# Moving softmax sums by DMA instead of transposing the attention outputs, in a fused FFN-attention-FFN layer

## The chip, the cores and the metric

The kernel runs on one core of one Trainium2 chip. The metric is the device time of one execution in microseconds, as the median of several runs. A profiled execution gives a trace beside it. In what follows PE is TensorE (matrix products and transposes by a product with the identity), DVE is VectorE, ACT is ScalarE, POOL is GpSimd, and SP is the queue from which most DMAs are issued. Each engine works its own instructions in program order.

## The reference, cut to what matters

The input `x` has 16 batches of 256 tokens with 256 features. The layer is

```
x = x + 0.5 * ffn(layernorm(x))        # 256 -> 1024 -> 256, ternary weights, exact gelu
x = x + attention(layernorm(x))        # 16 heads of 16, rotary, causal
x = x + 0.5 * ffn(layernorm(x))

q, k, v = x @ Wq.T, x @ Wk.T, x @ Wv.T      # heads of 16, q and k rotated
scores  = where(causal, q k^T / 4, -inf)
out     = softmax(scores) v                 # per head
return out @ Wo.T
```

All arithmetic is float32; the FFN splits its activations into a rounded part and a rest, so that two fast products stand for one exact one.

## The kernel before, in words

All tokens stay in SBUF (`xs`, 8 blocks of 512 tokens). The first FFN runs in 66 steps (8 blocks times 8 chunks of the hidden width, plus two): a step multiplies up one chunk (`up`), takes gelu twice on ACT, subtracts to get the rest on DVE or POOL (`h_rest`), and multiplies down the chunk of two steps before (`down`). The second FFN is alike.

Attention is a pipeline over batches, written out by hand in `slot(b, p)`: turn `b` has eight slots `p`. In one slot the scores of two heads of batch `b` are computed for their row maxima (tile `m`), and the transposed scores of two heads of batch `b - 1` for the weights (tile `w`). DVE takes the masked maxima out of `m`, adds the causal mask to `w`, and ACT takes exp into `pT`. Around the scores each slot holds another piece: turning the maxima (`turn_max`), the projections of the next batch (`project_qk`, `project_v`, `turn_x`), the rotary step on POOL (`rotate`, whose pairs of rows are swapped by two DMAs), `spread` on ACT, and what belongs to finished batches: `attend`, `divide`, `turn_out`, `project_out`, `add_out`, `last_stats`. The wrapper `InOrder` keeps every engine, SP's DMAs too, in the order in which the program is written. Since all instructions pass through it, the profile puts nearly everything on line 167, and groups are told apart by their tiles.

PSUM is shared by three pools of two tiles: `ps_w` (tile `w`, also the FFN's output), `ps_m` (tile `m`; a slot uses both), and `ps_mm` for all the rest. So a slot's maxima must be taken before the next slot's scores can be written, and a `mm` tile must be copied out before the next but one is begun.

`attend(b, half)` multiplies the weights with `vals`. Each head has 32 columns there: 16 values, a one, and zeros. The product therefore carries the head's outputs in 16 rows and the sum of its weights in a 17th. ACT copies it to `avs`. `divide(b, half)` transposes `avs` by four products with the identity, so that tokens lie in rows, takes the reciprocal of the 16 sums of a token and multiplies (tile `o`). `turn_out(b)` transposes `o` back by four more, and `project_out(b)` multiplies with `wo`. In `slot`, `attend` stands at slots 0 and 4, `divide` at 2 and 5, `turn_out` at 5, `project_out` at 7.

The list `head` lays the first projections and the first turn (`slot(0, 0..7)`) over the last 14 steps of the first FFN. After the last turn, a block of eight slots with weights alone (`ahead`, `behind`) finishes the last two batches, and `tail` finishes the last one inside the second FFN's first steps.

## Time and profile before

| | |
|---|---|
| median of 3 runs | 629.41 us (627.12 to 629.56) |
| the profiled execution's own time | 627.33 us |
| its span, first to last instruction | 625.5 us |
| first FFN | to about 166 us |
| attention, steady turns of 20.25 us | about 168 to 473 us |
| last two batches | 473 to 490 us |
| second FFN | from about 488 us |
| DVE busy in 300 to 325 us | 20.4 of 25 us |
| ACT busy in 300 to 325 us | 18.2 of 25 us |
| POOL busy in 300 to 325 us | 14.2 of 25 us |

A row of the groups gives the engine, the operation, output and input tiles, shapes, count, then busy time and the mean of one, then the engine's idle time just before them and what ended it. Rows in order of time give start, length, engine, operation and count. A product's rows overlap, because products are pipelined: their cost is the distance of their starts.

### The profile page before, as it was taken

Reading aid. Unit: us, or ns where it says so; the run is one execution under the profiler, and the core shown is the slowest. Engines: PE = TensorE matmul, PEld = TensorE weight load, DVE = VectorE, ACT = ScalarE, POOL = GpSimd, SP = SyncE. Lnnn points to the kernel's source line nnn. Section 1 sums busy time; section 2 is a strip of 40 time slices with the busy share of each in tenths; the row PEclk is TensorE's granted clock in tenths of the full one; section 3 lists DMA queues with packets and bytes.
Section 4 is the critical chain, followed back from the end, with each engine's and each line's share of the span. In section 5 each row is a group of like instructions: output and inputs, shape, how many; then the busy total and the mean of one; then the engine's idle time right before and its main releaser. Section 6 shows DMA issues by size and latency. Waiting matters only on the chain.

```text
span 625.5 us, 14708 instructions
## 1 busy us (share of the span) xinstructions
PE 601.8 (96%) x5580; PEld 488.6 (78%) x5580; DVE 463.6 (74%) x1658; ACT 414.5 (66%) x714; POOL 298.4 (48%) x270
## 2 busy tenths in 40 slices
PE   3999999989899999999999999999998999999997
PEld 3798999977677777777777777777766798888886
DVE  6877888865687988888888888888886465555553
ACT  3667666763567677767767676767765666766674
POOL 3545566572464466445654556453430243333343
PEclk9999999998999999999999999999999999999999
DMA  9800000000000001100100001100100011010001
GB/s 285 176 20 1 2 1 2 0 35 18 19 36 36 20 19 37 36 20 19 37 36 29 27 20 36 37 19 20 36 3 3 1 35 35 34 36 32 25 23 57
DMA packets 25478, 21.30 MB, mean 34 GB/s; under 512 B 10944, under 2 KB 21056, under 8 KB 25408
## 3 DMA queue, kind: packets, MB, share of 16 engines
q1 hardware_dynamic: 24848, 19.44, 9.9%
q8 instruction: 44, 0.72, 0.5%
q10 hardware_dynamic: 560, 0.92, 0.4%
q14 instruction: 26, 0.21, 0.1%
HBM read 7.51 MB, written 4.19 MB: 19 GB/s over the span
## 4 chain that ended last, share of the span: by engine, by line
PE 90%; DVE 5%; ACT 2%; issue 1%; DMA 1%; POOL 1%; DVEq 0%; SPq 0%; POOLq 0%
PE mm L167 37%; PE w L167 30%; PE m L167 23%; DMA w<-in_w1T_dram 1%; DVE h_rest L167 1%; DVE w2q L167 1%; ACT h_high L167 1%; DVE xn L167 0%; ACT h_whole L167 0%; DVE w L167 0%; DVE xn_a L167 0%; ACT pT L167 0%; DVE totals L167 0%; DVE st L167 0%; DVE w1q L167 0%
## 5 line engine op out<-in xcount | busy, mean ns | idle before, releaser
L167 DVE CUSTOM_DVE_ANT_0 masked<-m,mask_q 128x128 f32<-128x128 f32 x480 | 142.8, 353 | 40.5 <-PE m L167 39.3
L167 PE MATMUL m<-xnT,w1q 128*128 128x512 f32 x512 | 146.7, 408 | 1.1 <-DVE w1q L167 1.0
L167 ACT ACTIVATE h_high<-m,b_sb 128x512 fp32r<-128x512 f32 x128 | 88.1, 688 | 81.8 <-PE m L167 81.8
L167 DVE TENSOR_TENSOR h_rest<-h_whole,h_high 128x512 fp32r<-128x512 f32 x86 | 78.0, 908 | 73.3 <-ACT h_whole L167 72.8
L167 ACT ACTIVATE pT<-w 128x768 f32<-128x768 f32 x128 | 104.2, 814 | 30.3 <-DVE w L167 24.4
L167 PE MATMUL w<-qT,kT 32*128 32x256 f32 (+1 forms) x1024 | 121.1, 348 | 2.6 <-ACT pT L167 1.6
L167 PE MATMUL w<-w2q,h_high 128*128 128x256 f32 x480 | 121.4, 287 | 0.1
L167 PE MATMUL w<-w2q,h_rest 128*128 128x256 f32 x480 | 118.4, 280 | 1.3 <-DVE h_rest L167 1.3
L167 PEld LDWEIGHTS w<-qT,kT 32*128 32x128 f32 x1024 | 90.4, 184 | 34.1 <-issue 26.1
L167 PE MATMUL m<-kT,qT 32*128 32x128 f32 x960 | 114.9, 349 | 0.7 <-ACT kT L167 0.7
L167 POOL TENSOR_TENSOR h_rest<-h_whole,h_high 128x512 fp32r<-128x512 f32 x42 | 55.9, 1332 | 106.8 <-ACT h_whole L167 106.6
L167 PEld LDWEIGHTS m<-xnT,w1q 128*128 128x128 f32 x512 | 89.0, 192 | 17.5 <-DVE xnT L167 2.8
L167 PEld LDWEIGHTS w<-w2q,h_rest 128*128 128x128 f32 x480 | 91.0, 190 | 5.8 <-DVE h_rest L167 1.7
L167 DVE TENSOR_TENSOR w<-w,mask_k 128x512 f32<-128x512 f32 x128 | 88.8, 695 | 7.9 <-PE w L167 7.7
L167 PEld LDWEIGHTS w<-w2q,h_high 128*128 128x128 f32 x480 | 90.9, 189 | 4.5 <-DVE w2q L167 0.8
L167 ACT ACTIVATE h_whole<-m,b_sb 128x512 f32<-128x512 f32 x128 | 87.1, 681 | 0.0
L167 PEld LDWEIGHTS m<-kT,qT 32*128 32x128 f32 x960 | 66.0, 185 | 2.6 <-ACT kT L167 1.3
L167 POOL TENSOR_TENSOR w<-w,cosT 128x512 f32<-128x512 f32 x32 | 40.8, 1276 | 51.0 <-ACT w L167 33.1
L167 PE MATMUL mm<-xnT_a,wqk 128*128 128x256 f32 x256 | 62.2, 386 | 0.0
L167 POOL TENSOR_SCALAR var<-mv 128x4 f32<-128x4 f32 (+1 forms) x32 | 8.6, 268 | 109.6 <-DVE mv L167 109.1
L167 POOL TENSOR_TENSOR w<-w,sinT 128x512 f32<-128x512 f32 x32 | 41.3, 1291 | 32.5 <-DMA w<-w 32.5
L167 PEld LDWEIGHTS mm<-xnT_a,wqk 128*128 128x128 f32 x256 | 46.1, 190 | 7.6 <-issue 0.7
(86 smaller groups left out, 915.7 us busy)
## 6 DMA issues: line engine op xcount, KB each, us to landing
w<-w SPq DMA_DIRECT2D x64, 128.0 KB
out_dram<-x SPq DMA_DIRECT2D x15, 256.0 KB
x<-in_x_dram SPq DMA_DIRECT2D x7, 512.0 KB
w<-in_w2T_dram SPq DMA_DIRECT2D x1, 1024.0 KB
qT<-mT SPq DMA_DIRECT2D x64, 4.0 KB
w<-in_w1T_dram SPq DMA_DIRECT2D x1, 512.0 KB
w<-in_w1T_dram ACTq DMA_DIRECT2D x1, 512.0 KB
wqk<-in_wqkvT_dram SPq DMA_DIRECT2D x16, 32.0 KB
```

Source lines behind the costliest of these rows:

```text
L167: return tc.keep_in_program_order(getattr(self.engine, name)(*args, **kwargs))
```

## The change

Outputs are no longer turned to have tokens in rows. `vals` is filled with ones, and for every second group of four heads the 16 values lie in columns 16 to 31 instead of 0 to 15, the ones in the other half. So the product of `attend` has a head's outputs in 16 rows and its sum, repeated, in 16 rows beside them. ACT copies the product to `avs` as before and a second copy of its first half to `o`. Per batch, twelve DMAs of 16 rows (four in `gather` for each of three kinds) bring the outputs of a half together in `o` and the sums to the same rows in `over`, a part of the buffer that held the second weights. `divide`, called once a batch, takes the reciprocal of `over` (128x512) and multiplies it with `o` into `oT`, which is laid out for `project_out` at once. `wo` is loaded in the matching order of rows by eight DMAs. `turn_out` is gone, and so are the transposes of `divide`.

`gather` is issued in slots 0 to 3 of turn `b + 2`, `divide` runs in slot 1 of turn `b + 3`, `project_out` in slot 6 and `add_out` in slot 7 of that turn. `turn_x` moves from slot 6 to 2, `project_v` from 2 and 6 to 5 and 7, `project_qk`'s first half is split over slots 1 and 2, and `rotate` moves from slots 2 to 5 to slots 3 to 6. The head begins at step 40 instead of 46 and 52, its rotations are spread over steps 47 to 55, and the first turn begins at step 59 instead of 58, its last slot behind the FFN. In block 6 of the first FFN three `h_rest` move from DVE to POOL, and the addition of the bias moves to a later step.

```diff
-        nc.gpsimd.memset(v, 0.0)
-        nc.gpsimd.memset(v[:, :, :, HD : HD + 1], 1.0)
+        nc.gpsimd.memset(v, 1.0)
...
-            engine = gpsimd if f in (1, 3, 5) and not (ln == 0 and i >= NBLK - 2) else vector
+            engine = gpsimd if f in (1, 3, 5) and not (ln == 0 and i == NBLK - 1) else vector
...
-                if f == (0 if ln == 0 and i >= NBLK - 2 else 1 if ln == 2 and i == NBLK - 1 else 6):
+                if f == (1 if i == NBLK - 1 else 6):
                     add_bias(i)
...
-        scalar.copy(vals[b % 2][:, c, :, 0:HD], v.rearrange("p (h d) -> p h d", d=HD))
+        heads = "p (j e r d) -> p e j r d"
+        to = vals[b % 2][:, c].rearrange("p (j e r) d -> p e j r d", j=2, e=2)
+        for e in range(2):
+            scalar.copy(
+                to[:, e, :, :, e * HD : (e + 1) * HD],
+                v.rearrange(heads, j=2, e=2, d=HD)[:, e],
+            )
...
-        sums[b, half] = pp.tile([P, 2, S], FP, name="avs")
-        scalar.copy(sums[b, half], av)
...
+            sums[b] = pp.tile([P, 2, 2, S], FP, name="avs")
+            o[b] = pp.tile([P, 2, S], FP, name="o")
+        scalar.copy(sums[b][:, half], av)
+        scalar.copy(o[b][:, half, :], av[:, 0, :])
+
+    def gather(b, strips):
+        over[b] = spare[b % 2]
+        for r in strips:
+            first, second = (slice(at, at + HD) for at in (32 * r, 32 * r + HD))
+            sync.dma_start(out=over[b][first], in_=sums[b][second, :, 0, :])
+            sync.dma_start(out=over[b][second], in_=sums[b][first, :, 1, :])
+            sync.dma_start(out=o[b][second], in_=sums[b][second, :, 1, :])
+
+    def divide(b):
+        oT[b] = pp.tile([P, KC, S], FP, name="oT")
+        vector.reciprocal(over[b], over[b])
+        vector.tensor_mul(oT[b], o[b], over[b])
...
         if p == 0 and last is not None:
             attend(last, 1)
+            gather(last, (0,))
...
-            slots = VALUES.get(n, (2, 6))
+            slots = VALUES.get(n, (5, 7))
...
+        if p in (1, 2, 3) and up is not None:
+            project_qk(up, p // 3, {1: (0,), 2: (1,), 3: (0, 1)}[p])
+        if p in (1, 2, 3) and last is not None:
+            gather(last, (p,))
+        if p in (3, 4, 5, 6) and up is not None:
+            rotate(up, (p - 3) // 2, (p - 3) % 2)
...
-        if p == 6 and b + 2 < NB:
+        if p == 2 and b + 2 < NB:
             turn_x(b + 2)
+        if p == 6 and out is not None:
+            project_out(out, 0)
+            project_out(out, 1)
...
-        if p == 2 and last is not None:
-            divide(last, 1)
-        if p == 5 and past is not None:
-            divide(past, 0)
+        if p == 1 and out is not None:
+            divide(out)
...
+    head = {
+        40: lambda: ready_x(0, vector),
+        42: lambda: turn_x(0),
+        43: lambda: ready_x(1, vector),
+        44: lambda: project_qk(0, 0),
+        47: lambda: rotate(0, 0, 0),
+        48: lambda: (rotate(0, 0, 1), turn_x(1)),
+        50: lambda: project_qk(0, 1),
+        52: lambda: (rotate(0, 1, 0), spread(0, 0, 0)),
+        53: lambda: spread(0, 0, 1),
+        55: lambda: rotate(0, 1, 1),
+        56: lambda: ready_x(2, vector),
+    }
+    HEAD = 59
...
     ahead = {
-        0: lambda: (turn_max(z, 1), attend(a, 1)),
-        4: lambda: turn_out(a),
+        0: lambda: (turn_max(z, 1), attend(a, 1), gather(a, (0, 1, 2, 3))),
+        3: lambda: (project_out(y, 0), project_out(y, 1)),
         5: lambda: attend(z, 0),
-        6: lambda: project_out(a),
+        7: lambda: (project_out(a, 0), project_out(a, 1)),
     }
     behind = {
-        2: lambda: (divide(a, 1), last_stats(NB - 3)),
-        7: lambda: (add_out(a), last_stats(a), divide(z, 0)),
+        0: lambda: divide(y),
+        1: lambda: last_stats(y - 1),
+        4: lambda: add_out(y),
+        5: lambda: divide(a),
+        6: lambda: last_stats(y),
+        7: lambda: (add_out(a), last_stats(a)),
     }
...
     tail = [
-        lambda: attend(z, 1),
-        lambda: divide(z, 1),
-        lambda: turn_out(z),
-        lambda: project_out(z),
+        lambda: (attend(z, 1), gather(z, (0, 1, 2, 3))),
...
+        lambda: divide(z),
+        lambda: (project_out(z, 0), project_out(z, 1)),
         lambda: (add_out(z), last_stats(z)),
     ]
```

More of the change, by code (lines that the diff above doesn't have):

```diff
@@ L109 @@
             )
-    nc.sync.dma_start(out=wo, in_=woT.rearrange("(k p) f -> p k f", p=P))
+    for r in range(4):
+        for e in range(2):
+            at, to = 4 * HD * e + HD * r, 32 * r + HD * e
+            nc.sync.dma_start(
+                out=wo[to : to + HD, :, :],
+                in_=woT.rearrange("(k p) f -> p k f", p=P)[at : at + HD],
+            )
     nc.sync.dma_start(out=cos_sb, in_=rope_c.rearrange("(c p) d -> p c d", p=P))
@@ L409, in after_first @@
         later.extend(todo)
-    xn_a, xnT, qT, kT, o, oT, y_a = {}, {}, {}, {}, {}, {}, {}
-    pT, sums = {}, {}
+    xn_a, xnT, y_qk, qT, kT, o, oT, y_a = {}, {}, {}, {}, {}, {}, {}, {}
+    pT, sums, over = {}, {}, {}
     raw, pair = (
@@ L419 @@
     )
-    qk = [flat2[:, at : at + 2 * S].rearrange("p (n s) -> p n s", n=2) for at in (0, 2 * S)]
+    qk, spare = (
+        [flat2[:, at : at + 2 * S].rearrange("p (n s) -> p n s", n=2) for at in (k, k + 2 * S)]
+        for k in (0, 4 * S)
+    )
     def ready_x(b, engine=gpsimd):
@@ L436, in turn_x, with project_qk @@
         scalar.copy(xnT[b], tp)
-    def project_qk(b, j):
-        to = ps_mm.tile([P, 2, S], FP, name="mm")
-        for n in range(2):
+    def project_qk(b, j, parts=(0, 1)):
+        if 0 in parts:
+            y_qk[b, j] = ps_mm.tile([P, 2, S], FP, name="mm")
+        to = y_qk[b, j]
+        for n in parts:
             for k in range(KC):
@@ L449, in project_qk @@
                 )
+        if 1 not in parts:
+            return
         scalar.copy(raw[j], to)
@@ L483, in project_v @@
             )
-        scalar.copy(vals[b % 2][:, c, :, 0:HD], v.rearrange("p (h d) -> p h d", d=HD))
+        heads = "p (j e r d) -> p e j r d"
+        to = vals[b % 2][:, c].rearrange("p (j e r) d -> p e j r d", j=2, e=2)
+        for e in range(2):
+            scalar.copy(
+                to[:, e, :, :, e * HD : (e + 1) * HD],
+                v.rearrange(heads, j=2, e=2, d=HD)[:, e],
+            )
     def turn_max(b, j):
@@ L574, in attend @@
                     )
-        sums[b, half] = pp.tile([P, 2, S], FP, name="avs")
-        scalar.copy(sums[b, half], av)
-    def divide(b, half):
         if half == 0:
-            o[b] = pp.tile([P, 2, H, HD], FP, name="o")
-        tp = ps_mm.tile([P, 2, 8, 32], FP, name="mm")
-        for c in range(2):
-            for n in range(2):
-                tensor.transpose(
-                    tp[:, c, 4 * n : 4 * n + 4, :].rearrange("p h d -> p (h d)"),
-                    sums[b, half][:, n, c * P : (c + 1) * P],
-                    ident,
-                )
-        inv = pp.tile([P, 2, 8, 1], FP, name="inv")
-        vector.reciprocal(inv, tp[:, :, :, HD : HD + 1])
-        vector.tensor_mul(
-            o[b][:, :, 8 * half : 8 * half + 8, :],
-            tp[:, :, :, 0:HD],
-            inv.to_broadcast([P, 2, 8, HD]),
-        )
@@ L598, in turn_out @@
-    def turn_out(b):
-        tp = ps_mm.tile([P, KC, S], FP, name="mm")
-        for k in range(KC):
-            for c in range(2):
-                tensor.transpose(
-                    tp[:, k, c * P : (c + 1) * P],
-                    o[b][:, c, 8 * k : 8 * k + 8, :].rearrange("p h d -> p (h d)"),
-                    ident,
-                )
-        oT[b] = pp.tile([P, KC, S], FP, name="oT")
-        scalar.copy(oT[b], tp)
-    def project_out(b):
-        y = y_a[b] = ps_mm.tile([P, 2, D], FP, name="mm")
-        for c in range(2):
-            for k in range(KC):
-                tensor.matmul(
-                    y[:, c, :],
-                    oT[b][:, k, c * P : (c + 1) * P],
-                    wo[:, k, :],
-                    start=(k == 0),
-                    stop=(k == KC - 1),
-                )
+            sums[b] = pp.tile([P, 2, 2, S], FP, name="avs")
@@ new lines, in divide, with project_out @@
+    def divide(b):
+        oT[b] = pp.tile([P, KC, S], FP, name="oT")
+        vector.reciprocal(over[b], over[b])
+        vector.tensor_mul(oT[b], o[b], over[b])
+    def project_out(b, c):
+        if c == 0:
+            y_a[b] = ps_mm.tile([P, 2, D], FP, name="mm")
+        for k in range(KC):
+            tensor.matmul(
+                y_a[b][:, c, :],
+                oT[b][:, k, c * P : (c + 1) * P],
+                wo[:, k, :],
+                start=(k == 0),
+                stop=(k == KC - 1),
+            )
@@ L640, in slot @@
         up, now, past, last = (n if 0 <= n < NB else None for n in (b + 1, b, b - 1, b - 2))
-        if p == 0 and 0 <= b - 3 < NB:
-            add_out(b - 3)
+        out = b - 3 if 0 <= b - 3 < NB else None
+        if p == 7 and out is not None:
+            add_out(out)
         weigh = scores(bw, p, bm, p ^ 1)
@@ L645, in slot @@
             attend(last, 1)
+            gather(last, (0,))
         if p == 1 and past is not None:
             turn_max(past, 1)
-        if p == 5:
-            if now is not None:
-                turn_max(now, 0)
-            if last is not None:
-                turn_out(last)
+        if p == 5 and now is not None:
+            turn_max(now, 0)
         for n, at in ((past, p + 8), (now, p)):
-            slots = VALUES.get(n, (2, 6))
+            slots = VALUES.get(n, (5, 7))
             if n is not None and at in slots:
                 project_v(n, slots.index(at))
-        if p in (1, 3) and up is not None:
-            project_qk(up, p // 2)
-        if p in (2, 3, 4, 5) and up is not None:
-            rotate(up, p // 2 - 1, p % 2)
+        if p in (1, 2, 3) and up is not None:
[4 more added lines that the diff above has]
+            rotate(up, (p - 3) // 2, (p - 3) % 2)
         if p == 4 and past is not None:
             attend(past, 0)
-        if p == 6 and b + 2 < NB:
+        if p == 2 and b + 2 < NB:
             turn_x(b + 2)
+        if p == 6 and out is not None:
+            project_out(out, 0)
+            project_out(out, 1)
         if p == 7:
-            if last is not None:
-                project_out(last)
             if b + 3 < NB:
@@ L673, in slot @@
         weigh()
-        if p == 2 and last is not None:
-            divide(last, 1)
-        if p == 5 and past is not None:
-            divide(past, 0)
-        if p == 0 and 0 <= b - 3 < NB:
-            last_stats(b - 3)
+        if p == 1 and out is not None:
+            divide(out)
+        if p == 0 and 0 <= b - 4 < NB:
+            last_stats(b - 4)
         for n, at in ((up, {7: (0, 1)}), (now, {2: (1, 0), 3: (1, 1)})):
@@ L685, in slot @@
             later.pop(0)()
-    head = [
-        lambda: (turn_x(0), ready_x(1, vector)),
-        lambda: project_qk(0, 0),
-        lambda: (rotate(0, 0, 0), project_qk(0, 1)),
-        lambda: (turn_x(1), rotate(0, 0, 1), rotate(0, 1, 0), ready_x(2, vector)),
-        lambda: rotate(0, 1, 1),
-        lambda: (spread(0, 0, 0), spread(0, 0, 1)),
-    ] + [lambda p=p: slot(0, p) for p in range(8)]
+    head = {
[12 more added lines that the diff above has]
+    HEAD = 59
     begin, step, *_ = ffn(0, after_first)
@@ L702 @@
         step(u)
-        if u == (NBLK - 3) * NFC + 6:
-            ready_x(0, vector)
-        if u >= FFN_STEPS - len(head):
-            head[u - (FFN_STEPS - len(head))]()
+        head.get(u, lambda: None)()
+        if u >= HEAD:
+            slot(0, u - HEAD)
+    for p in range(FFN_STEPS - HEAD, 8):
+        slot(0, p)
     for b in range(1, NB - 1):
@@ L734 @@
     a, z = NB - 2, NB - 1
-    add_out(NB - 3)
+    y = NB - 3
     ahead = {
-        0: lambda: (turn_max(z, 1), attend(a, 1)),
-        4: lambda: turn_out(a),
+        0: lambda: (turn_max(z, 1), attend(a, 1), gather(a, (0, 1, 2, 3))),
+        3: lambda: (project_out(y, 0), project_out(y, 1)),
         5: lambda: attend(z, 0),
-        6: lambda: project_out(a),
+        7: lambda: (project_out(a, 0), project_out(a, 1)),
     }
     behind = {
-        2: lambda: (divide(a, 1), last_stats(NB - 3)),
-        7: lambda: (add_out(a), last_stats(a), divide(z, 0)),
+        0: lambda: divide(y),
[4 more added lines that the diff above has]
+        7: lambda: (add_out(a), last_stats(a)),
     }
@@ L751 @@
     tail = [
-        lambda: attend(z, 1),
-        lambda: divide(z, 1),
-        lambda: turn_out(z),
-        lambda: project_out(z),
+        lambda: (attend(z, 1), gather(z, (0, 1, 2, 3))),
+        lambda: None,
+        lambda: None,
+        lambda: None,
+        lambda: None,
+        lambda: divide(z),
+        lambda: (project_out(z, 0), project_out(z, 1)),
         lambda: (add_out(z), last_stats(z)),
```

## The prediction, made before the result was known

> **What bounds the kernel now.** I read the page's engine row and chain first.

> ```profile
> PE 601.8 (96%) x5580; PEld 488.6 (78%) x5580; DVE 463.6 (74%) x1658; ACT 414.5 (66%) x714; POOL 298.4 (48%) x270
> ...
> PE 90%; DVE 5%; ACT 2%; issue 1%; DMA 1%; POOL 1%; DVEq 0%; SPq 0%; POOLq 0%
> ```

> TensorE (PE) sets the end, but only as long as its in-order queue never waits. The stage that changes is attention, so next I read PE in order of time over one batch's turn (start, length):

> ```profile
> 301.11 0.48 PE L167 MATMUL w<-qT,kT 32*128 32x256 f32 x1
> ...
> 301.98 1.51 PE L167 MATMUL mm<-pT,vals 128*32 128x256 f32 x32
> 303.42 0.48 PE L167 MATMUL w<-qT,kT 32*128 32x256 f32 x1
> ...
> 304.29 0.44 PE L167 MATMUL mm<-ident,maxes 128*128 128x128 f32 x2
> 304.56 0.60 PE L167 MATMUL mm<-ident,o 128*128 128x128 f32 x4
> 305.19 0.66 PE L167 MATMUL mm<-ident,avs 128*128 128x128 f32 x4
> 305.77 0.48 PE L167 MATMUL w<-qT,kT 32*128 32x256 f32 x1
> ```

> Starts tell the cost, since the ends overlap: the scores of a slot take 0.87 us (301.11 to 301.98), attend 1.44, two maxes' transposes 0.27, four transposes about 0.56 (0.58 here, 0.53 elsewhere). The same list gives 0.97 for project_v, 1.92 for eight wqk or wo products. The turn is 20.25 us (301.11 to 321.36), all PE work. VectorE (DVE) in the same slots, and its groups:

> ```profile
> 303.20 0.69 DVE L167 TENSOR_TENSOR w<-w,mask_k 128x512 f32<-128x512 f32 x1
> 304.39 0.29 DVE L167 CUSTOM_DVE_ANT_0 masked<-m,mask_q 128x128 f32<-128x128 f32 x1 [0.49 <-PE m L167]
> ...
> 306.11 0.25 DVE L167 RECIPROCAL inv<-mm 128x16 f32<-128x16 f32 x1
> 306.39 0.42 DVE L167 TENSOR_TENSOR o<-mm,inv 128x256 f32<-128x256 f32 x1
> ```

> ```profile
> L167 DVE CUSTOM_DVE_ANT_0 masked<-m,mask_q 128x256 f32<-128x256 f32 x240 | 100.7, 420 | 0.0
> ...
> L167 DVE CUSTOM_DVE_ANT_0 masked<-m,mask_q 128x128 f32<-128x128 f32 x240 | 68.7, 286 | 40.5 <-PE m L167 39.3
> ...
> L167 DVE RECIPROCAL inv<-mm 128x16 f32<-128x16 f32 x32 | 7.9, 247 | 0.8 <-PE mm L167 0.8
> ```

> A slot asks DVE for four masked maxima (1.12 us, 302.08 to 303.20) and one mask addition (0.60), 1.72 in all. The pool of `m` has two tiles and a slot uses both, so PE's scores of slot p+1 cannot begin before DVE has read slot p's. Slots last 2.3 to 3.0 us: DVE has only 0.5 to 1.0 us to spare in each. A long DVE instruction stops PE.

> **What the change removes.** Twelve transposes a batch go (eight of `avs`, four of `o`): 3 x 0.56 = 1.7 us of PE. Summing the new slots 0 to 7 (scores, then attend; maxes + half wqk; half wqk + turn_x; full wqk; attend; maxes + project_v; wo; project_v): 2.31 + 2.10 + 2.37 + 2.79 + 2.31 + 2.12 + 2.80 + 1.85 = 18.65 us, 1.6 below 20.25. From DVE two short divisions go (2 x 0.65, start to start).

> **What it adds on DVE.** One reciprocal of 128x512 and one product of 128x512, back to back behind slot 1's mask addition. The product is like the 128x512 addition: 0.69. Call the reciprocal R. The trace has it only for 16 elements: 247 ns. Other DVE instructions that read PSUM have a fixed part near 150 ns (286 ns at 128 elements and 420 at 256 make 1.05 ns an element, leaving 152; a 128x1 operation on PSUM takes 151). The remaining 97 ns over 16 elements is 6.1 ns an element, so R = 0.15 + 512 x 6.1 ns = 3.26 us. From below: if the 97 ns are a latency paid once, R = 0.15 + 512 x 1.05 ns = 0.69 (0.8 with it). [...]

> **What this does to a turn.** Let T0 be the start of slot 0's scores. Masked maxima start 0.95 after a slot's scores. Slot 0: they end at 2.07, mask addition 2.67, last_stats 1.08 (as at 313.62 to 314.70): DVE free at 3.75. Slot 1 starts at 2.31, its maxima could start at 3.26 but do at 3.75; they end 4.87, mask addition 5.47, then R + 0.69: DVE free at 6.16 + R. Slot 2's scores have run meanwhile, their maxima end at 7.28 + R, and slot 3's scores are held until about 0.12 before that (w products go first). Without waits slot 3 starts at 2.31 + 2.10 + 2.37 = 6.78. So PE stands still for 7.16 + R - 6.78 = 0.38 + R in slots 1 to 2. Slot 7 is now so short (1.85, with add_out's 0.69 before its maxima) that slot 0 waits another 0.1. The turn is 18.65 + 0.1 + 0.38 + R = 19.13 + R. The same reckoning on the kernel before gives 20.25, as measured. With R = 3.26 it is 22.39, +2.14 us; 13 turns (b = 3 to 15) have a division: **+27.8 us**. Queued behind the reciprocal are the masked maxima (PE waits), slot 2's mask addition and thus its exp on ScalarE.

> **The clock.** Before the first turn, PE idled 1.35 and 1.90 us close together and then ran at half clock (columns: stretch, length, busy of the engines, granted clock):

> ```profile
> 140.00:141.00 1.00, 0.00 (x0) 0.00 (x0) 1.00 (x2) 0.00 (x0) 1.00 (x1) 1.00 0.00 0
> 141.00:142.00 1.00, 0.70 (x8) 0.55 (x8) 0.75 (x2) 0.00 (x0) 0.07 (x1) 1.00 0.00 0
> 142.00:143.00 1.00, 1.00 (x5) 0.73 (x3) 0.74 (x5) 0.00 (x0) 0.00 (x0) 0.65 0.00 0
> 143.00:144.00 1.00, 1.00 (x4) 0.74 (x3) 0.46 (x4) 0.00 (x0) 0.00 (x0) 0.50 0.00 0
> 144.00:145.00 1.00, 1.00 (x7) 1.00 (x6) 0.00 (x0) 0.84 (x2) 0.00 (x0) 0.50 0.00 0
> 145.00:146.00 1.00, 1.00 (x8) 0.78 (x9) 0.54 (x1) 0.42 (x1) 0.00 (x0) 0.65 0.00 0
> ```

> That is about 3.4 us at half, 1.7 us lost. [...] The row shows that partly idle stretches suffice. [...]

> **What it adds elsewhere.** ScalarE: two more copies of 128x256 in attend (2 x 0.37), project_v's copy in two pieces (about 0.27 each for 0.37), less oT's copy (0.585): +0.5 us on some 14 busy in 20; the exp waits for DVE anyway, so 0. If that cover is gone, 0.5 x 14 = 7 us. SP: twelve more DMAs a turn. Issues of the pair and qT DMAs take about 0.55 us each, so 6.6 us of a queue that issued eight a turn. Three go into each of slots 0 to 3, ahead of a pair or qT DMA, which is at most 1.65 us late; pair DMAs land 2.7 us after issue (316.95 to 319.65), the rotation is a slot later and spread in slot 7, so 0 here. The sums are divided a turn after they were moved: 0. GpSimd's moved rotations: 0 in the steady turn.

> **Head, first turns, end.** The head's stalls before the first turn (1.35 + 1.90 + 1.65 of half clock = 4.9) come from DVE behind two xn_a normalizations slowed to 2.67 us and h_rest at 4.59 for two, all beside GpSimd's rotations. Those spread over steps 40 to 56, three h_rest go to GpSimd, and the scores start a step later: **-4** (-5 to +2; GpSimd's sum of 17 us in eleven steps of 1.9 is near full). Turns 1 and 2 lose four and twelve transposes and wo's 1.92, which goes into the last block: -0.53 - 3.53 = **-4.1**. The last block (eight slots of scores alone, 472.7 to 489.4): two reciprocals stand in it; following mask addition, exp and the two `w` tiles slot by slot, its last exp ends 19.9 us after its start instead of 16.7: **+3.3**. Tail: eight transposes less (-1.1), a DVE block of 3.9 us at step 5 against some 3 us of slack of h_rest (+0.6): **-0.5**.

> Sum: 27.8 + 10.4 - 4 - 4.1 + 3.3 - 0.5 = +32.9 on the profiled execution's 627.3 (span 625.5): **660 us**. The runs' median is 629.4, 0.3% above it, inside the spread.

> **Rivals.** *A fast reciprocal* (R = 0.69): turn 19.82, 13 x -0.43 = -5.6, no half clock, last block -1, the rest -8.6: -15, **612 us**. For it: a latency could explain 97 ns. Against: no other short row has 80 ns more. Break-even lies at 13 (R - 1.12) + 1.67 (R - 0.68) - 1 = 8.6, R = 1.7 us, 3 ns an element. [...] *No clock loss at R = 3.26*: **650**; it belongs to my likeliest case. *Late DMAs:* if the pair DMAs behind three gathers cost 1.65 us in each of 14 turns, +23: **683**; SP's idle time and the slack above speak against it. *In between* (R = 1.4 to 2.2): 623 to 640.

> **How the numbers follow.** R near 3.3 with or without the clock: 0.62, 650 to 672. Eight cycles: 0.15. Fast: 0.14. In between: 0.06, half of it the same as before. Late DMAs: 0.03. Leaving out the fast case below and the extremes above gives 638 to 684. A measurement here tells about 0.5% from no change: faster 0.15, same 0.03, slower 0.82.

> **What would show it.** RECIPROCAL 128x512 near 3.3 us; an idle PE of about 3 us in slot 2 to 3 of each turn, released by DVE `maxes`; turns of 22 to 23.5 us; dips of the granted clock in attention; no SP wait on the way; PE matmuls fewer by 192. A reciprocal under 1.7 us makes the forecast wrong.

## The result, and the profile after

The changed kernel takes 724.55 us (median of 4 runs, 723.64 to 726.30) against 629.23 us for the kernel before (4 runs beside it): 1.152 times as long, with a 95% interval of 1.148 to 1.155. The forecast was 660, with a range of 638 to 684. The direction was right; the slowdown was three times the one forecast.

The engine row and the chain's row of the page after:

```profile
PE 652.8 (90%) x5388; PEld 503.8 (70%) x5388; DVE 503.2 (70%) x1623; ACT 414.7 (57%) x762; POOL 302.0 (42%) x271
...
PE 69%; DVE 15%; ACT 5%; DMA 4%; issue 2%; SPq 2%; POOL 1%; DVEq 0%; POOLq 0%
```

PE has 192 products fewer and is yet busy 51 us longer, which says that products ran more slowly. On the chain DVE has gone from 5% to 15%, ACT from 2% to 5%. The two new groups on DVE:

```profile
L174 DVE RECIPROCAL w<-w 128x512 f32<-128x512 f32 x16 | 53.5, 3342 | 0.0
...
L174 DVE TENSOR_TENSOR oT<-o,w 128x512 f32<-128x512 f32 x16 | 11.2, 699 | 0.5
```

So R = 3.34 us, where 3.26 was forecast, and 0.70 for the product. The disputed term was right. To find where the rest went, the two traces are laid side by side at five marks: the transposes of the maxima in slot 1 of batches 1 and 3, the last scores for maxima, and the first `up` product of the second FFN.

| stretch | before | after | difference | forecast |
|---|---|---|---|---|
| start to slot 1 of batch 1 | 171.27 | 169.07 | -2.2 | -4 |
| turns 1 and 2 | 41.57 | 40.57 | -1.0 | -4.1 |
| turns 3 to 15, to the last scores for maxima | 257.04 | 348.83 | +91.8 | +38.2 |
| from there to the second FFN (last block) | 18.20 | 23.45 | +5.3 | +3.3 |
| second FFN | 137.42 | 140.58 | +3.2 | -0.5 |
| sum (spans 625.5 and 722.5) | | | +97.0 | +32.9 |

The turns hold nearly all of it. A steady turn lasts 27.30 us (from one reciprocal to the next, 348.12 to 375.42), 7.05 more than before; 2.94 were forecast. One stop of PE in order of time, first PE, then DVE (start, length, the idle time before and what ended it in brackets):

```profile
350.00 0.69 PE L174 MATMUL w<-qT,kT 32*128 32x256 f32 x2
352.79 0.37 PE L174 MATMUL m<-kT,qT 32*128 32x128 f32 x1 [2.10 <-DVE maxes L174]
...
354.93 3.78 PE L174 MATMUL mm<-xnT_a,wqk 128*128 128x256 f32 x8
```

```profile
348.12 3.34 DVE L174 RECIPROCAL w<-w 128x512 f32<-128x512 f32 x1
351.49 0.69 DVE L174 TENSOR_TENSOR oT<-o,w 128x512 f32<-128x512 f32 x1
352.10 0.28 DVE L174 CUSTOM_DVE_ANT_0 masked<-m,mask_q 128x128 f32<-128x128 f32 x1
...
375.42 3.34 DVE L174 RECIPROCAL w<-w 128x512 f32<-128x512 f32 x1
```

PE's slot 3 begins at 350.00 and stops, until DVE, behind the reciprocal and the product, takes the maxima of slot 2 from 352.10 on. PE resumes at 352.79. This is the wait that was forecast, in its place; its idle time is 2.10 us by PE's products and 2.50 by its weight loads, where 0.38 + R = 3.7 was reckoned. But the eight `wqk` products after it take 3.7 us (354.93 to the next start at 358.64). In the kernel before they took 1.93:

```profile
319.43 1.99 PE L167 MATMUL mm<-xnT_a,wqk 128*128 128x256 f32 x8
321.36 0.48 PE L167 MATMUL w<-qT,kT 32*128 32x256 f32 x1
```

The windows of the changed kernel over the same time (stretch, length, busy of PE, PEld, DVE, ACT and POOL, granted clock, DMA share and GB/s) tell why:

```profile
351.00:352.00 1.00, 0.00 (x0) 0.00 (x0) 0.97 (x2) 0.00 (x0) 0.59 (x1) 1.00 0.26 54
...
353.00:354.00 1.00, 1.00 (x13) 0.74 (x12) 0.90 (x3) 0.06 (x1) 0.02 (x1) 0.58 0.47 156
354.00:355.00 1.00, 1.00 (x8) 0.35 (x3) 0.39 (x3) 1.00 (x2) 1.00 (x1) 0.50 0.18 41
...
359.00:360.00 1.00, 1.00 (x16) 0.92 (x12) 0.00 (x0) 1.00 (x3) 0.00 (x0) 0.51 0.00 0
360.00:361.00 1.00, 1.00 (x26) 0.64 (x24) 0.75 (x5) 0.93 (x3) 0.00 (x0) 1.00 0.35 131
```

After the wait PE runs at a granted clock of 0.50 for about 6.8 us (353.15 to 359.98), in which it does 3.4 us of work: up to 3.4 us lost, in every turn, where the forecast had 0.8. A second wait is new and was not in the forecast at all. Slot 0 begins late (PE, then ACT):

```profile
342.68 0.37 PE L174 MATMUL m<-kT,qT 32*128 32x128 f32 x1 [0.79 <-ACT kT L174]
```

```profile
341.30 0.43 ACT L174 COPY vals<-mm 128x128 f32<-128x128 f32 x2 [1.24 <-PE mm L174]
341.62 0.52 ACT L174 ACTIVATE qT<-w,own 128x256 f32<-128x256 f32 x1
342.03 0.60 ACT L174 ACTIVATE kT<-w,one,own 128x256 f32<-128x256 f32 x1
```

The scores of a new batch need `kT`, which `spread(up, 0, 0)` writes in slot 7. There it stands behind the two copies of `vals`, and these wait for `project_v`, which now runs in slot 7. Slot 7 itself has become short (1.85 us). PE's idle at this place is 0.79 us by its products and 1.2 by its weight loads.

### The profile page after: what moved, and what is told of

The parts are those of the page before. It is cut to its first block, busy times and chain, and to the rows that moved or that the text cites. A ratio compares the mean times of both kernels' runs of the same rounds, so it can differ in the third digit from the quotient of the medians.

```text
span 722.5 us, 14732 instructions
## 1 busy us (share of the span) xinstructions
PE 652.8 (90%) x5388; PEld 503.8 (70%) x5388; DVE 503.2 (70%) x1623; ACT 414.7 (57%) x762; POOL 302.0 (42%) x271
## 4 chain that ended last, share of the span: by engine, by line
PE 69%; DVE 15%; ACT 5%; DMA 4%; issue 2%; SPq 2%; POOL 1%; DVEq 0%; POOLq 0%
PE mm L174 27%; PE m L174 21%; PE w L174 21%; DVE w L174 8%; DMA w<-avs 3%; SPq L174 2%; DVE oT L174 1%; DVE masked L174 1%; ACT kT L174 1%; ACT qT L174 1%; ACT vals L174 1%; DMA w<-in_w1T_dram 1%; ACT avs L174 1%; ACT h_high L174 1%; DVE w2q L174 1%
## 5 line engine op out<-in xcount | busy, mean ns | idle before, releaser
L174 PE MATMUL m<-kT,qT 32*128 32x128 f32 x960 | 144.5, 392 | 39.7 <-DVE maxes L174 29.3
L174 PE MATMUL w<-qT,kT 32*128 32x256 f32 (+1 forms) x1024 | 153.4, 385 | 4.9 <-ACT pT L174 4.0
L174 PEld LDWEIGHTS w<-qT,kT 32*128 32x128 f32 x1024 | 104.3, 204 | 46.4 <-issue 27.8
L174 PEld LDWEIGHTS m<-kT,qT 32*128 32x128 f32 x960 | 84.0, 210 | 57.4 <-DVE maxes L174 41.1
L174 DVE TENSOR_TENSOR h_rest<-h_whole,h_high 128x512 fp32r<-128x512 f32 x83 | 71.2, 858 | 73.9 <-ACT h_whole L174 73.4
L174 POOL TENSOR_TENSOR h_rest<-h_whole,h_high 128x512 fp32r<-128x512 f32 x45 | 60.1, 1336 | 109.4 <-ACT h_whole L174 109.2
L174 PE MATMUL mm<-xnT_a,wqk 128*128 128x256 f32 x256 | 87.6, 490 | 0.0
L174 PEld LDWEIGHTS mm<-xnT_a,wqk 128*128 128x128 f32 x256 | 57.9, 242 | 22.0 <-ACT pT L174 7.2
```

Of the source, the lines that this page charges most:

```text
L174: return tc.keep_in_program_order(getattr(self.engine, name)(*args, **kwargs))
```

## The experiments

Theory: the length of one DVE instruction in one slot stops PE (R + 0.48 a turn), and the stop halves PE's clock for some microseconds after it; slot 0's wait on `kT` comes on top. Rivals: the twelve DMAs are late; ScalarE's added copies; DVE's sum of work; the half clock comes from something else.

### The reciprocal made short, `spread` made early, and both

`e1_r16` inverts only 16 of the 512 columns, so the outputs are multiplied with sums instead of their inverses; `e2_spread6` lays `spread` one slot earlier; `e4_r16_spread6` has both.

```diff
-        vector.reciprocal(over[b], over[b])
+        vector.reciprocal(over[b][:, 0, 0:16], over[b][:, 0, 0:16])
```

```diff
-            if up is not None:
-                spread(up, 0, 0)
+        if p == 6 and up is not None:
+            spread(up, 0, 0)
```

> The changed kernel, but the reciprocal takes only 16 of the 512 columns (the other sums are left as they are, so the output is not the layer's). Theory: the reciprocal of 3.34 us causes both the wait of TensorE in slots 2 and 3 and the two windows of half clock behind it. Then its turn falls from 27.3 us to 19.13 + 0.25 by the prediction's formula plus 1.2 for the new wait of slot 0 on kT, about 20.6 us, the granted clock in attention is 1.00, and the whole takes about 628 us. Rival (the twelve DMAs or the moved pieces are the cost): the turn stays above 25 us and the whole above 695 us.

> The changed kernel with the first spread of the next batch in slot 6 instead of 7, so that slot 0's scores of maxima need not wait for kT behind the copies of the values. If the parts of a turn simply add, the turn falls by 1.2 us to 26.1 and the whole by 16 us to about 708 us. [...]

> Both: reciprocal of 16 columns only (output not the layer's) and the first spread in slot 6. By the formula 19.13 + 0.25 = 19.4 us a turn, TensorE never long idle, whole about 613 us: the most that the freed TensorE time could have given with a short division. Rival (a further wait is hidden in the new order of slots): turn above 20.2 us, whole not below 625 us.

Measured, in one execution each: 638.2, 693.8 and 623.3 us. The reciprocal's length alone is worth 86 us. Without it, and with `spread` early, the turns are shorter than in the kernel before, though all twelve DMAs, both copies and all other moves are there. The turn in `e1_r16`, then the turn and its windows in `e4_r16_spread6`:

```profile
253.89 0.24 DVE L174 RECIPROCAL w<-w 128x16 f32<-128x16 f32 x1
...
274.95 0.24 DVE L174 RECIPROCAL w<-w 128x16 f32<-128x16 f32 x1
```

```profile
250.92 0.24 DVE L174 RECIPROCAL w<-w 128x16 f32<-128x16 f32 x1
...
270.58 0.24 DVE L174 RECIPROCAL w<-w 128x16 f32<-128x16 f32 x1
```

```profile
270.00:280.00 10.00, 10.00 (x121) 7.27 (x118) 8.10 (x41) 7.60 (x14) 4.61 (x5) 1.00 0.28 82
280.00:290.00 10.00, 10.00 (x125) 7.32 (x129) 9.06 (x42) 6.91 (x15) 6.39 (x7) 1.00 0.08 18
```

A turn takes 21.06 us in the first and 19.66 in the second (250.92 to 270.58), so the wait on `kT` costs 1.40 us. In the second PE is busy all the time at full clock, 0.59 us a turn faster than the kernel before. So the turns are near the 20.6 and 19.4 that were expected. The whole times are not: both lie 10 us above the theory. In `e1_r16` the turns and a second FFN of 140.4 us explain most of it; in `e4_r16_spread6` there is half clock from 449.9 to 456.7 in the last turn, and twice more in the last block.

`e2_spread6` did not agree with the expectation that the parts add (26.1, and 708 for the whole): its turns last 24.40 or 25.9 us, 1.64 and 3.1 more than the 22.76 that the long reciprocal alone gives (19.66 + 3.10). One and the same kernel has one half-clock stretch in some turns (24.40) and two in others (25.9); a turn of 24.40 shows one half-clock stretch of about 3.4 us (a granted clock of 0.90, 0.50, 0.50, 0.50 and 0.90 in the five windows of 1 us from 339 to 344).

### PE kept busy during the wait

`e3_warm` and `e6_warm6` add products whose result nobody reads, at the end of slot 2 (twelve and six calls; each is two instructions):

```diff
+    def idle(b):
+        to = ps_mm.tile([P, 2, D], FP, name="mm")
+        for n in range(6):
+            tensor.matmul(
+                to[:, n % 2, :], ident, wo[:, n % 2, :], start=True, stop=True
+            )
...
+        if p == 2 and out is not None:
+            idle(b)
```

> The changed kernel with twelve 128x256 products that nobody reads at the end of slot 2, where TensorE otherwise waits for the maxima behind the reciprocal. They keep it busy for about 2.9 us. Theory (half clock follows from the wait): no half clock behind slot 2, the turn falls by 3.4 us to about 23.9 us or a little more, the whole to 675 to 690 us, although more work is done. Rival (the clock is lowered by something else, such as the whole load, or the products only add): the turn stays or grows, 725 us or more.

> The changed kernel with six products of ident with wo (512 columns in all a pair, result unused) at the end of slot 2, where PE would stand still for the reciprocal; half of what overshot the wait before (twelve took 5.4 us), so about 2.7 us and inside the wait of about 3.8. Theory (idle PE brings the half clock, and the half clock is worth 3.4 us a turn): turn 27.30 - 3.4 = 23.9, clock 1.00 in attention, whole about 680, though PE has more to do. Rival (the loss is not the clock but the wait itself): turn stays at 27.3, whole about 724. If six products still let PE stand 1.1 us, one window at half may remain: turn 25.6, whole about 702.

Measured, in one execution each: 713.9 and 687.2 us, the granted clock 1.00 in turns 3 to 15 in both. Twelve calls took 5.4 us and overshot the wait: their turn is 26.51 us. Six took 2.8 and fit:

```profile
334.05 3.34 DVE L174 RECIPROCAL w<-w 128x512 f32<-128x512 f32 x1
...
358.21 3.34 DVE L174 RECIPROCAL w<-w 128x512 f32<-128x512 f32 x1
```

The turn is 24.16 us in place of 27.30 with more work in it. This is the clock's price, with nothing of the reciprocal or its wait taken away: 3.14 us a turn. It also closes the ladder, each turn measured: 19.66, and 1.40 for `kT` makes 21.06; 3.10 for the whole reciprocal, which is the difference of the lengths 3.34 and 0.24, makes 24.16; 3.14 for the clock makes 27.30.

### The reciprocal alone in the kernel before

`e5_before_recip` puts only the long reciprocal into the kernel before, on a buffer that nobody reads:

```diff
+    def block():
+        late = flat2[:, 6 * S : 8 * S]
+        vector.reciprocal(late, late)
...
+        if p == 1 and 0 <= b - 3 < NB:
+            block()
```

> The kernel before with nothing of the change but one reciprocal of 128x512 (on a part of the second weights' buffer that nobody reads) in slot 1 of turns 3 to 15; output unaffected. Theory (the reciprocal stops PE, and the stop brings half clock): reckoned slot by slot as in the prediction, the turn is 22.4 us without clock loss (+2.2, thirteen turns +28) and one or two windows at half clock (1.7 or 3.4 us) come on top: turns of 24.1 to 25.9, the whole 680 to 705, granted clock in attention about 0.9. Rival (the half clock comes from the other moves, such as the wait on kT): turn 22.4, clock near 1.00, whole about 658. Rival (the reciprocal hurts only in the new arrangement of slots): turn under 21, whole under 640.

Measured, in one execution: 684.2 us. Three of its reciprocals:

```profile
366.30 3.34 DVE L167 RECIPROCAL w<-w 128x512 f32<-128x512 f32 x1
...
390.43 3.34 DVE L167 RECIPROCAL w<-w 128x512 f32<-128x512 f32 x1
...
412.92 3.34 DVE L167 RECIPROCAL w<-w 128x512 f32<-128x512 f32 x1
```

The turns are 24.13 and 22.49 us. The short one is the only one of eleven without a half-clock stretch, and it is the 22.4 that was reckoned without one; the others have one stretch of 3.4 us, 1.64 us lost. So one DVE instruction of 3.34 us brings both losses without any other part of the change. PE's idle time ahead of the half clock is small here, 1.0 us by its products and 1.4 by its weight loads, and it is the same in the turn that escaped. PE in a turn with half clock and in that one:

```profile
370.20 0.37 PE L167 MATMUL m<-kT,qT 32*128 32x128 f32 x1 [1.02 <-DVE maxes L167]
...
394.33 0.37 PE L167 MATMUL m<-kT,qT 32*128 32x128 f32 x1 [1.02 <-DVE maxes L167]
```

### The DMAs left out, and half a reciprocal

`e10_no_dma` moves no sums; `e11_r256` inverts 256 columns.

```diff
-        for r in strips:
+        for r in ():
```

> The changed kernel without the twelve DMAs a batch (the sums are not moved, the output is wrong); all instructions of the engines stand. Rival (late DMAs: SP's queue holds the pair and qT DMAs back and so PE): 10 to 23 us less, 700 to 715. Theory (reciprocal, clock and the wait on kT only): 722 to 726, turn 27.3.

> The changed kernel with the reciprocal over 256 of the 512 columns (the other half of the outputs is multiplied by sums, so the output is wrong). R becomes 0.15 + 256 x 6.2 ns = 1.75 us and the wait in slot 2 about 0.4 + 1.75 = 2.1. By the wait alone the turn is 21.06 (with 16 columns) + 1.5 = 22.6 at most, whole about 655; with one window at half clock 1.7 more, 24.3 (7 windows are 23.9), whole about 678; with two, 26.0, whole about 700. I take one window, since the kernel before with an added reciprocal lost one at a wait of about 2.0.

`e10_no_dma` takes 725.1 us (one execution), with turns of 27.30:

```profile
430.89 3.34 DVE L174 RECIPROCAL w<-w 128x512 f32<-128x512 f32 x1
...
458.19 3.34 DVE L174 RECIPROCAL w<-w 128x512 f32<-128x512 f32 x1
```

The DMAs cost nothing in the turns of the changed kernel, although its chain gives DMA and SPq 6% of the span, some 43 us. A place on the chain is not a price.

`e11_r256` takes 671.5 us (one execution), between the cases of no window (655) and one (678). Its turns tell more: eight of eleven steady ones last 22.56 us, what the wait alone gives (21.06, and 1.74 - 0.24 for the longer reciprocal), and three last 24.18, one half-clock stretch more. PE's wait on the maxima is at most 0.5 us by its products and 0.9 by its weight loads there.

### The reciprocal in pieces

If only the length in one slot matters, the same work in pieces must be free in the turns. `e7_pieces` cuts the reciprocal in seven, over slots 5 to 7 of one turn and 1 to 4 of the next, and gives the multiplication to POOL:

```diff
     def divide(b):
         oT[b] = pp.tile([P, KC, S], FP, name="oT")
-        vector.reciprocal(over[b], over[b])
-        vector.tensor_mul(oT[b], o[b], over[b])
+        gpsimd.tensor_mul(oT[b], o[b], over[b])
+
+    def invert(b, at, n):
+        part = over[b].rearrange("p n s -> p (n s)")[:, at : at + n]
+        vector.reciprocal(part, part)
...
+        for n, at in ((last, {5: (0, 48), 6: (48, 96), 7: (144, 32)}), (out, {1: (176, 48), 2: (224, 80), 3: (304, 112), 4: (416, 96)})):
+            if n is not None and p in at:
+                invert(n, *at[p])
+        if p == 4 and out is not None:
+            divide(out)
```

> The changed kernel with spread one slot earlier, the multiplication on POOL and the reciprocal cut in seven pieces of 32 to 112 columns over slots 5 to 7 of one turn and 1 to 4 of the next, so that each fits into what a slot leaves of DVE; the same sums, the same arithmetic. Theory (only the length of one DVE instruction in one slot matters, not its sum): reckoned slot by slot 19.8 to 20.0 us a turn, clock 1.00, whole 625 to 635, with the last block still slow. Rival (DVE's total is the bound: its 3.3 us more a turn cost wherever they stand): turn about 22.5, whole about 665. Rival (the DMAs or ScalarE's copies are the loss): turn stays above 25.

Measured: 687.9 us, 1.091 times the kernel before (1.085 to 1.098). A miss, but not by a cause that the theory or a rival named. The trace has a new wait:

```profile
348.04 1.65 PE L174 MATMUL mm<-wv,xnT_a 128*128 128x256 f32 x4 [2.49 <-ACT o L174]
```

```profile
347.61 0.37 ACT L174 COPY o<-mm 128x256 f32<-128x256 f32 x1 [2.65 <-POOL oT L174]
```

The tile `o` has two buffers. ACT's copy for one batch waits until POOL has multiplied that of two batches before, POOL's multiplication stands behind rotations that wait for their DMAs, and PE needs the `mm` tile that the copy empties. `e9_pieces2` therefore has three tiles of `o`, and six pieces, the first of them later (slots 6 and 7). To make room, the scratch tile `masked` was cut to one buffer.

```diff
-            o[b] = pp.tile([P, 2, S], FP, name="o")
+            o[b] = pp.tile([P, 2, S], FP, name="o", bufs=3)
...
-                        out=pp.tile([P, S], FP, name="masked")[:, 0:cols],
+                        out=pp.tile([P, S], FP, name="masked", bufs=1)[:, 0:cols],
```

> As the kernel in seven pieces, with its two own waits mended: the first piece stands two slots behind the last gathering DMA (slots 6 and 7 of one turn: 112 and 48 columns; slots 1 to 4 of the next: 48, 80, 112, 112), and the tile o has three buffers in place of two, so that ScalarE's copy in slot 4 does not wait for POOL's multiplication of two batches before; in the last block the reciprocals are cut too. Theory: reckoned slot by slot 19.9 us a turn, clock 1.00, whole 622 to 632. Rival (the DMAs and the moved pieces cost by themselves whatever the reciprocal does): turn above 22, whole above 655.

Measured: 680.5 us (1.081, 1.078 to 1.084), full clock, but turns of 22.67. The four masked maxima of a slot:

```profile
302.56 0.28 DVE L174 CUSTOM_DVE_ANT_0 masked<-m,mask_q 128x128 f32<-128x128 f32 x1
...
302.88 0.42 DVE L174 CUSTOM_DVE_ANT_0 masked<-m,mask_q 128x256 f32<-128x256 f32 x1
...
303.45 0.29 DVE L174 CUSTOM_DVE_ANT_0 masked<-m,mask_q 128x128 f32<-128x128 f32 x1
...
303.79 0.42 DVE L174 CUSTOM_DVE_ANT_0 masked<-m,mask_q 128x256 f32<-128x256 f32 x1
```

They start 0.32, 0.57 and 0.34 us apart, where the kernel before has about 0.22, 0.34 and 0.21. With one scratch tile each starts only after the one before has ended, although its content is never read. That is 0.45 us a slot, and in the windows from 280 to 330 DVE is busy 9.0 to 9.3 of 10 us and hardly waits for anybody. The wait comes from the program: all four write one tile. `e12_pieces3` gives `masked` its two tiles again, with which the four start 0.21, 0.35 and 0.21 us apart (from 302.89), and takes the room from `oT` (one tile).

> As the kernel in seven pieces with three tiles of o, but with two tiles for the unused output of the masked maxima again (one tile made each of the four wait for the one before: they started 0.32, 0.57 and 0.34 us apart instead of 0.22, 0.34 and 0.21, which is 0.45 us a slot, and DVE became the bound at 22.67 us a turn) and one tile of oT. Theory (the length of one DVE instruction in one slot is the loss, not DVE's sum): reckoned slot by slot 19.9 us a turn, clock 1.00; thirteen times 2.8 less than the last one, 645, and less half clock in the last block: 630 to 646. Rival (DVE's sum, which rises by 4.2 us a turn, is the bound wherever the pieces stand): turn above 21.5, whole above 660.

Measured: 635.65 us (1.009, 1.006 to 1.012), with turns of 19.56 us at best. Two windows of such turns:

```profile
300.00:310.00 10.00, 10.00 (x122) 7.50 (x118) 9.48 (x40) 8.43 (x17) 7.24 (x7) 1.00 0.28 82
310.00:320.00 10.00, 10.00 (x126) 7.20 (x119) 9.74 (x47) 6.45 (x14) 5.33 (x6) 1.00 0.08 17
```

DVE is busy 9.5 to 9.8 us in each stretch of 10 from 300 to 360, where it was 8.2 in the kernel before, and PE is busy all the time. So DVE's sum was not the loss. But only six of the twelve turns from batch 3 on last 19.4 to 19.6; the others last up to 21.4, and PE waits for POOL's `oT` in them (5.0 us in four waits). Their mean is 20.04, against 20.25 before. What remained above 629 lay in the last block (24.95 us between the marks, 18.20 before) and in the second FFN (141.75, 137.42 before), with a wait of 3.8 us on `oT`.

`e13_pieces4` divides the last two batches in pieces inside the second FFN's first 15 steps, and halves POOL's multiplication:

```diff
+        1: lambda: last_stats(y),
+        2: lambda: invert(a, 0, 128),
+        3: lambda: (invert(a, 128, 128), divide(a, 0)),
...
+        9: lambda: (project_out(a, 0), project_out(a, 1)),
...
+        18: lambda: (project_out(z, 0), project_out(z, 1)),
```

> As the last kernel in pieces, with three more moves: POOL's multiplication in two halves (after slots 2 and 4); in the last block only the batch before the last two is divided, in four pieces, and projected in slot 6; the last two batches are divided in pieces of 128 columns in steps 2 to 15 of the second FFN, where DVE is half idle, and projected in its steps 9 and 18. Theory (the last block and the tail lost by the same means as the turns, a long reciprocal in DVE's queue): last block near the 15.4 us of the kernel before in place of some 22, no wait of 3.8 us in the second FFN, turns 19.56: 635.7 less some 9, 622 to 630. Rival (the block and the tail lose by the DMAs' way, or by ScalarE, or by half clock that comes anyway): block above 20 us, whole 632 to 638.

Measured: 626.98 us, 0.997 times the kernel before (0.995 to 0.999). Its engine row:

```profile
PE 594.6 (95%) x5388; PEld 470.6 (75%) x5388; DVE 493.1 (79%) x1682; ACT 415.6 (67%) x762; POOL 324.9 (52%) x303
```

This is the only version of the change, with all of its work done, that is below the kernel before, by 0.3%, which is less than the 0.5% that was called distinguishable. The last block takes 20.3 us between the marks (24.95 in `e12_pieces3`), still more than the 18.2 of the kernel before; the second FFN, which now holds two projections, takes 140.8. The turns from batch 3 on last 19.83 in the mean, 0.4 less than before. By the marks, the stretch up to batch 3 and the turns gain 6.3 us, and the last block and the second FFN lose 5.7 again.

### The head alone

`e8_head` is the kernel before with only the head's new list, the three subtractions moved to POOL and the later bias.

```diff
+    head = {
+        40: lambda: ready_x(0, vector),
+        42: lambda: turn_x(0),
...
+    HEAD = 59
```

> The kernel before with only the change's head list (first projections and rotations over more steps, first turn a step later), the three more subtractions on POOL and the later bias. The prediction gave this -4 us (-5 to +2); between the two profiles the first turn's marker moved by -2.2. Theory: 1.5 to 3.5 us faster, 626 to 628, no half clock before the first turn. Rival: the head of the changed kernel gained only through its other parts: within 0.5 us of 629.4.

Measured: 0.996 times the kernel before (0.994 to 0.999), that is -2.3 us on 629.78. It agrees with the -2.2 between the two profiles. Where the gain lies is not shown: the one trace of this kernel is of an execution of 634.27 us, with half clock for 10.2 us from 142.6 on.

## Why the prediction was right and wrong

**Right: the reciprocal's price.** "R = 0.15 + 512 x 6.1 ns = 3.26": it measured 3.342, and over the lengths run (0.24 for 16 columns in SBUF, 0.64 for 80, 1.743 for 256, 3.342 for 512) 0.14 us + 6.25 ns an element. The row of 16 elements (247 ns) gave the price of 512 within 2.5%.

**Right: the wait.** "PE stands still ... for 0.38 + R": the turn without half clock was reckoned as 19.13 + R. With 16 columns and `spread` early it is 19.66 (19.13 + 0.24 = 19.37 reckoned), in the kernel before with the reciprocal 22.49 (22.4 reckoned). The base was 0.29 too low. That R goes into the turn in full is shown by three lengths: 0.24, 1.74 and 3.34 us give turns of 21.06, 22.56 and 24.16 without half clock. PE's idle time in this one place is shorter than reckoned (2.10 or 2.50 in place of 3.7); the trace also has waits of 0.26 us on the maxima around it, and the rest was not followed up.

**Wrong: the clock.** This step failed. The sum's +10.4 us is 0.8 a turn over thirteen turns; that was my estimate, and no run shows it. What `e6_warm6` measured is 3.14 a turn. The row of the kernel before showed one stretch of half clock, 3.41 us long with 1.7 us lost, and I took one as the most; in the changed kernel two such stretches follow each other in every steady turn (6.83 us). And idle time of 1.0 us by PE's products (1.4 by its weight loads) was followed by half clock in ten of eleven turns of `e5_before_recip`. Over thirteen turns the step's miss is 13 x (3.14 - 0.8) = 30 us, about half of the miss of 64.

**Wrong: nothing elsewhere.** "spread in slot 7, so 0 here" and "Slot 7 is now so short ... that slot 0 waits another 0.1". `spread` is done by ACT behind `project_v`'s copies, and I costed the copies by their own length, not by whom they hold back. This step failed too: the wait that was put at nothing is 1.40 us a turn (21.06 against 19.66), 18 us over thirteen.

**The rest of the miss.** 13 x (0.29 + 0.08) = 5 us are the turn's base and R. The last block took 5.3 more instead of 3.3; with 16 columns it took 18.1 us in `e1_r16` and 19.7 in `e4_r16_spread6`, against 23.45, so most of this is the long reciprocals again. The second FFN took +3.2 instead of -0.5: PE waits 2.95 us for `oT`, and half clock follows (a granted clock of 0.50 from 598.91 to 602.33). Here the slack of "some 3 us" was wrong. With 16 columns a wait of 2.0 remains: the product on DVE waits 0.5 for a DMA (`o` from `avs`) in `e1_r16` and lasts 2.23 us. Without the DMAs (`e10_no_dma`) the second FFN takes the same 140.6 as in the changed kernel, so they cost nothing beside the long reciprocal; whether they would bind with a short one is open. The head brought 2.2 of 4. Turns 1 and 2 brought 1.0 of the 4.1 expected; there too one wait on `kT` stands (0.79 us), but with `spread` early the sum of head and these turns stayed the same (209.25 against 209.64 to batch 3), so why they fell short is open.

**Rivals.** The fast reciprocal falls with R = 3.34. For "Eight cycles", which had 0.15, no run shows how long a cycle is; measured are 6.25 ns an element. Late DMAs fall with `e10_no_dma` for the turns. "No clock loss" (650) falls with the half clock in every turn; with PE kept busy the changed kernel takes 687, since the wait on `kT` (18 us) and the smaller misses above remain.

**The signs named.** A reciprocal near 3.3, a PE wait in slots 2 to 3 released by `maxes` (2.1 to 2.5 us in place of about 3), dips of the granted clock and 192 products fewer were all there. "Turns of 22 to 23.5" was not: 27.30. Nor was "no SP wait on the way": the chain has 2% of SP's queue and 4% of DMA, which cost nothing, as `e10_no_dma` shows.

## To carry to other kernels

Cost a long instruction by what queues behind it on its engine: 3.1 us more of DVE in one slot cost 6.2 us a turn (21.06 to 27.30), and the same arithmetic in six pieces, each fitted to the slack of its slot, with the multiplication on POOL, cost none in the best turns (19.57). Where PE is the bound, price a repeated wait of PE together with the half clock after it, which here was as dear as the wait (3.14 us a turn, against 3.10 for the reciprocal's whole length); filling the wait with idle products shows that price directly. And when a piece of work moves to a neighbouring slot, look at what it now stands in front of on every in-order queue, as here `project_v`'s copies before `kT` (1.40 us a turn).
